# The last attention's loop: heavy rows in the middle, expert pieces spread evenly, and half of the edge features added by the gathers

## The chip, the core and the metric

The kernel runs on one core of one Trainium2 chip. The core has five engines with a queue of instructions each: PE (TensorE, matrix products), DVE (VectorE), ACT (ScalarE), POOL (GpSimd) and SP (SyncE, which here only issues transfers). Sixteen DMA engines move the data. The metric is device time in microseconds; the kernel before was run three times, with a median of 5483.48 us (5478.16 to 5485.61).

## What is computed

Four graph layers alternate with four expert layers on 3125 nodes of 256 features. The change lies in the last two, an attention over 50,000 edges sorted by destination, and a mixture of eight experts:

```python
def _L3_gnn_ref(x, edge_index, edge_attr, Wq, bq, Wk, bk, Wv, bv, We, Ws, bs):
    q, k, v = ...                       # x @ W + b, as (n, 8, 32)
    e = (edge_attr @ We).reshape(-1, H, C)
    kj = k[src] + e
    alpha = jnp.einsum('ehc,ehc->eh', q[dst], kj) / jnp.sqrt(jnp.float32(C))
    ...                                 # softmax of alpha over the edges of a destination
    msg = (v[src] + e) * alpha[:, :, None]
    out = jax.ops.segment_sum(msg, dst, num_segments=n)
    return out.reshape(n, H * C) + (x @ Ws + bs)

def _L3_ffn_ref(x, ...):
    w = jax.nn.softmax(jnp.mean(x, axis=0) @ Wr + br, axis=-1)
    h = jax.nn.relu(_bn(jnp.einsum('bfd,edh->bfeh', x, W1) + b1, ...))
    h = jax.nn.relu(_bn(jnp.einsum('bfeh,ehk->bfek', h, W2) + b2, ...))
    y = jnp.einsum('bfeh,ehd->bfed', h, Wo) + bo
    return jnp.einsum('bfed,fe->bfd', y, w)
```

The edge's feature row `e` is added both to the key and to the value of the edge's source.

## The kernel before, in words

**Rows and groups.** Both layers are one loop, in `gnn3_rows` (from line 1294). The nodes were sorted by how many edges come in. A tile holds 128 nodes, one to a partition; a step of a tile takes one edge for each of its nodes. The 25 light tiles have 5 to 31 steps. Nodes with 32 edges or more have their edges cut into heavy rows of 32 steps; there are three tiles of them. In all there are 440 steps, taken in 66 groups of at most eight (`GW`). The sums of the heavy rows are joined (`many_join`) before the last three light tiles, the ones whose nodes have heavy rows too, are begun.

**A group.** `fetch` (line 1391) puts on POOL's queue: for a tile's first group one gather of its queries, one gather of the features of all the group's steps (`e_`, one contiguous stretch of E to a partition), and one gather for each step, of the key and value rows of the edges' sources, 2 KB a partition (`kv`). POOL works through its queue in order. `kv` has three buffers and `e_` two. `ahead` copies the features of a pair of steps to PSUM on ACT, and `add` (line 1419) adds them to key and value on DVE. Then DVE multiplies by the query and sums by head (L1669, L1672), works out the running maximum, and, after ACT's exponential, multiplies the values by the weights (L1694). PE sums the group's weighted values in PSUM by products with an identity (L1633), in `sum_up`, which is called in the middle of the next group and which also fetches the group after that.

**The experts.** The light tiles form units of four (the last ones of two and one). When all tiles of a unit have their attention, `next_layer` hangs a chain of small tasks on `todo` (norm, transpose, gate), of which a few are done in each group; at its end the unit's expert work is put on `slots` as pieces: a product of a layer's half (its PSUM bank is read by a relu on ACT, L1575), or a result of two tiles (read by DVE, L1590, which weighs it and adds it to the nodes). `add` takes pieces from `slots` as its account `room` allows: each step pays in 1.25 and each group 1.5, and each piece costs what is written beside it. What is left when the loop ends is done behind it. Each unit loads all experts' weights anew on SP's queue.

**What sets the order.** The loop is under a manual schedule: DVE, ACT, PE and POOL each run their instructions in the order in which the program writes them, and wait by semaphores for each other.

Of the kernel before, what the change touches and what calls it, by code (L numbers as in the profile page):

```python
# [9 lines left out]
F32 = mybir.dt.float32  # L10
BF16 = mybir.dt.bfloat16
I32 = mybir.dt.int32
U32 = mybir.dt.uint32
AF = mybir.ActivationFunctionType
ALU = mybir.AluOpType
# [4 lines left out]
P = 128  # L20
C = 256
KC = C // P
N = 3125
NT = 25
# [3 lines left out]
GW = 8  # L28
# [4 lines left out]
HB = 3  # L33
# [25 lines left out]
class Kernel:  # L59
# [1234 lines left out]
    def gnn3_rows(self):  # L1294
# [4 lines left out]
        nc, tc, a, S = self.nc, self.tc, self.a, self.S  # L1299
        H, dh = 8, 32  # L1300
        QX = self.dram.tile([NP, 2, C], F32, name="r3_QX")
        KV = self.dram.tile([NP, 2, C], F32, name="r3_KV")
        row_of = lambda x: x.rearrange("n i c -> n (i c)")
        heads = lambda x: x.rearrange("p (h d) -> p h d", h=H)
        with pool_of(tc, name="r3t", bufs=1) as sp, pool_of(tc, name="r3tp", bufs=2, space=PSUM) as pp:
            w = sp.tile([P, KC, 4, C], F32, name="w4")
            b = sp.tile([P, 4, C], F32, name="b4")
            for i, x in enumerate("qskv"):
                nc.sync.dma_start(out=w[:, :, i, :], in_=a["L3_gnn_W" + x].rearrange("(k p) f -> p k f", p=P))
                ap = a["L3_gnn_b" + x]  # L1310
# [41 lines left out]

        fb = NT - HN

        units = [list(range(t, t + 4)) for t in range(0, fb - 2, 4)] + [[fb - 2, fb - 1], [NT - 1, fb], [fb + 1]]
        order = [HB + t for u in units[:-3] for t in u] + list(range(HB)) + [HB + t for u in units[-3:] for t in u]
        steps = [(i, s0, n, g) for i in order for g, (i_, s0, n) in enumerate(S.groups) if i_ == i]
        pairs = [(q, j) for q, (_, _, n, _) in enumerate(steps) for j in range(0, n, 2)]
        first_pair = [pairs.index((q, 0)) for q in range(len(steps))]
        unit_of = {t: u for u in units for t in u}  # L1360
        M0 = -0.1 * BIG
        with pool_of(tc, name="r3v", bufs=2) as vp, pool_of(tc, name="r3vp", bufs=2, space=PSUM) as pp, \
# [8 lines left out]
            got, todo, done, mvs, joined = {}, [], set(), {}, set()  # L1371
# [9 lines left out]
            def bank(shape, name):  # L1381

                while behind and behind[0][0] <= made[0] - 3:
                    _, ps, read = behind.pop(0)
                    read(ps)
                made[0] += 1
                return pp.tile(shape, F32, name=name, tag="bank", bufs=3)

            misc = lambda shape: bank(shape, f"misc{shape[0]}_{shape[-1]}_{len(shape)}")

            def fetch(q):
                if q >= len(steps):
                    return
                i, s0, n, g = steps[q]
                kv = vp.tile([P, GW, 2, C], F32, name="kv", bufs=3)
                e = vp.tile([P, GW, C], F32, name="e_", bufs=2)
                qx = None
                if s0 == 0 and HB <= i < HB + fb:
                    qx = vp.tile([P, 2 * C], F32, name="qx", bufs=2)
                    self.gather(qx, row_of(QX), S.id[:, i - HB : i - HB + 1])  # L1400
                self.gather(e[:, :n, :].rearrange("p n c -> p (n c)"), self.E, S.at[:, g : g + 1])
                for j in range(n):
                    o = S.start[i] + s0 + j
                    self.gather(kv[:, j].rearrange("p i c -> p (i c)"), row_of(KV), S.src[:, o : o + 1])
                got[q] = kv, e, qx

            copies, room = {}, [0.0]

            def ahead(p):

                if p >= len(pairs):
                    return
                q, j = pairs[p]
                n = min(2, steps[q][2] - j)
                pe = pp.tile([P, 2, C], F32, name="pe", bufs=2)
                nc.scalar.copy(pe[:, :n, :], got[q][1][:, j : j + n, :])
                copies[p] = pe

            def add(q, j):
                n = min(2, steps[q][2] - j)  # L1420
                room[0] += n * 1.25
                while slots and room[0] > 0:
                    room[0] -= slot()
                if not slots:
                    room[0] = 0.0
                p = first_pair[q] + j // 2
                kv = got[q][0][:, j : j + n]
                nc.vector.tensor_tensor(kv, kv, copies.pop(p)[:, :n, :].unsqueeze(2).to_broadcast([P, n, 2, C]), ALU.add)  # L1428
                ahead(p + 2)

            def many_join():
# [110 lines left out]
            def load(i):  # L1542

                if i >= len(units) * E // 2 or i in weights_of:
                    return
                weights_of[i] = []
                for e in (i * 2 % E, i * 2 % E + 1):
                    w = wp.tile([P, 3, KC, C], F32, name="w")
                    for k, x in enumerate(("W1", "W2", "Wo")):
                        nc.sync.dma_start(out=w[:, k], in_=a["L3_ffn_" + x][e].rearrange("(k p) f -> p k f", p=P))  # L1550
                    weights_of[i].append(w)

            def experts(u, hold):

                n = len(u) * P
                at = units.index(u) * E // 2
                for pair in range(E // 2):
                    es_ = (2 * pair, 2 * pair + 1)
                    h = {}

                    def product(e, l, f, pair=pair, h=h):
                        if l == 0 and f == 0:
                            load(at + pair + e % 2)
                        w = weights_of[at + pair][e % 2]
                        if f == 0:
                            h[e, l] = hp.tile([P, KC, 4 * P], F32, name=f"hT{l}")
                        x = hold["zT"] if l == 0 else h[e, 0]
                        ps = bank([P, 4 * P], "fp")
                        for k in range(KC):
                            nc.tensor.matmul(ps[:, :n], w[:, l, k, f * P : (f + 1) * P], x[:, k, :n], start=(k == 0), stop=(k == KC - 1))  # L1570
                        return ps

                    def relu(ps, e, l, f, h=h):
                        c = e * KC + f
                        nc.scalar.activation(h[e, l][:, f, :n], ps[:, :n], AF.Relu, bias=self.bn3[l][1][:, c : c + 1], scale=self.bn3[l][0][:, c : c + 1])  # L1575

                    def result(e, j0, pair=pair, h=h):
                        w = weights_of[at + pair][e % 2]
                        ps = bank([P, 4 * P], "fp")
                        for j in range(j0, min(j0 + 2, len(u))):  # L1580
                            for k in range(KC):
                                nc.tensor.matmul(
                                    ps[:, (j - j0) * C : (j - j0 + 1) * C], h[e, 1][:, k, j * P : (j + 1) * P], w[:, 2, k, :],
                                    start=(k == 0), stop=(k == KC - 1))
                        return ps

                    def weigh(ps, e, j0):
                        for j in range(j0, min(j0 + 2, len(u))):
                            x = self.xs[:, u[j], :]
                            nc.vector.scalar_tensor_tensor(  # L1590
                                x, ps[:, (j - j0) * C : (j - j0 + 1) * C], hold["g"][:, j, e : e + 1], x, op0=ALU.mult, op1=ALU.add)
                        if e == E - 1 and j0 + 2 >= len(u):
                            later.extend(u)

                    for l in range(2):
                        for e in es_:
                            for f in range(KC):
                                yield n / 512 * 1.75, lambda e=e, l=l, f=f, g=product: g(e, l, f), lambda ps, e=e, l=l, f=f, g=relu: g(ps, e, l, f)
                    for e in es_:
                        for j0 in range(0, len(u), 2):  # L1600
                            yield min(2, len(u) - j0) * 0.87, lambda e=e, j0=j0, g=result: g(e, j0), lambda ps, e=e, j0=j0, g=weigh: g(ps, e, j0)

            def slot():

                cost, make, read_ = slots.pop(0)
                if len(behind) > 1:
                    _, ps, read = behind.pop(0)
                    read(ps)
                ps = make()
                behind.append((made[0] - 1, ps, read_))  # L1610
                return cost
# [8 lines left out]
                        in_=self.xs[:n, t, :], in_offset=None)  # L1620

            load(0)
            fetch(0)
            fetch(1)
            for p in range(2):
# [16 lines left out]
            for st, (i, s0, n, g_) in enumerate(steps):  # L1642
                kv, e_, qx = got[st]
                light = i >= HB
                t = i - HB
                last = s0 + n == S.sizes[i]
                if s0 == 0:
# [9 lines left out]
                    if light and t >= fb:  # L1657
                        assert joined == set(range(HN))
                        m, den, before = tot[:, t - fb, C + H :], tot[:, t - fb, C : C + H], tot[:, t - fb, :C]
                room[0] += 1.5  # L1660


                for k, j in enumerate(range(added, n, 2)):
                    if k == 2:
                        sum_up(st)
                    add(st, j)
# [3 lines left out]
                l = vp.tile([P, H, GW + 1], F32, name="l")  # L1670
                ln = l[:, :, 1 : n + 1]
                nc.vector.tensor_reduce(ln, k_.rearrange("p n (h d) -> p h n d", h=H), AX.X, ALU.add)  # L1672
                o = S.start[i] + s0
# [9 lines left out]
                e = es[st % 2]  # L1683
# [56 lines left out]
            while todo or slots or behind or later:  # L1740
# [5 lines left out]
                if behind and not slots and not todo:  # L1746
                    _, ps, read = behind.pop(0)
# [672 lines left out]
```

## Time and profile before

| | us |
|---|---|
| median of three runs | 5483.48 (5478.16 to 5485.61) |
| the profiled execution, its time | 5477.25 |
| its span, first to last instruction | 5475.5 |
| first kv gather of the loop, last kv gather, last sum of the loop (start) | 4406.7, 5349.3, 5383.2 |
| busy over the whole span: PE, DVE, ACT, POOL | 2901.7, 3425.3, 1055.9, 3030.6 |

A stage is a stretch of the span, in microseconds from its start; its row gives how long each engine was busy in it. A group of instructions is a source line on an engine with its operands, its count, its busy time and the mean duration of one, and then how long the engine stood idle ahead of it and what ended that. The mean granted clock of TensorE is 0.74 over the span. The loop is the last fifth of it: what comes before does not change.

### The profile page before, as it was taken

What the parts mean: (1) busy time and instruction counts of PE and PEld (TensorE: products, weight loads), DVE (VectorE), ACT (ScalarE), POOL (GpSimd) and SP (SyncE); (2) the same over time, 40 slices, a digit from 0 to 9 for tenths busy, and PEclk for the clock granted to TensorE, in tenths of its full rate; (3) what the DMA queues carried; (4) which work ended last, traced back from release to release, by engine and by line L of the source; (5) the groups of instructions that cost most, each with busy time, mean ns of one, the idle gap of its engine ahead of it and who ended that gap; (6) DMA issues with size and microseconds to landing.
All of it is one profiled execution on the core that took longest, in us unless ns stands there. A gap on an engine that the chain in (4) does not pass through costs nothing. (4 is left out here: it accounts for less than half of the span.)

```text
span 5475.5 us, 41427 instructions
## 1 busy us (share of the span) xinstructions
PE 2901.7 (53%) x10276; PEld 2038.4 (37%) x10276; DVE 3425.3 (63%) x7869; ACT 1055.9 (19%) x2359; POOL 3030.6 (55%) x3128
## 2 busy tenths in 40 slices
PE   2233326962333258433332332888881637989858
PEld 1222225851222135322222221555551224656537
DVE  5998752126888645688847777211113677988893
ACT  1111101211111112211111110222221023433324
POOL 3777633024777431677747775677774054545550
PEclk9665657986656579755566565799995868999969
DMA  5677626743777400577737774232321566767764
GB/s 194 202 249 274 238 84 199 223 150 99 259 256 267 143 16 6 170 261 260 260 116 245 249 252 158 70 95 82 88 74 53 186 208 199 248 212 249 247 206 128
DMA packets 417368, 982.05 MB, mean 179 GB/s; under 512 B 98494, under 2 KB 238856, under 8 KB 386262
## 3 DMA queue, kind: packets, MB, share of 16 engines
q0 software_dynamic: 159856, 446.40, 27.8%
q1 hardware_dynamic: 229526, 468.51, 24.0%
q10 hardware_dynamic: 27728, 64.32, 3.0%
q8 instruction: 87, 1.43, 0.1%
q14 instruction: 171, 1.40, 0.1%
HBM read 629.95 MB, written 348.99 MB: 179 GB/s over the span
## 5 line engine op out<-in xcount | busy, mean ns | idle before, releaser
L1264 PE MATMUL fe_p<-feat_we,fe_T 128*128 128x256 f32 x1564 | 630.7, 573 | 1316.1 <-ACT fe_T L1260 1316.0
L1264 PEld LDWEIGHTS fe_p<-feat_we,fe_T 128*128 128x128 f32 x1564 | 434.8, 291 | 1476.2 <-ACT fe_T L1260 1380.8
L153 POOL DMA_INDIRECT hg<-g_H,A_src x782 | 760.3, 972 | 242.9 <-issue 210.4
L940 DVE SCALAR_TENSOR_TENSOR hg<-hg,A_keep,v 128x264 f32<-128x264 f32 (+1 forms) x1368 | 666.3, 487 | 44.8
L153 POOL DMA_INDIRECT hg<-f_H,B_src x512 | 520.0, 1016 | 156.1 <-issue 155.8
L153 POOL DMA_INDIRECT kv<-r_KV,r_src x440 | 417.9, 950 | 323.5 <-PE acc L1633 186.1
L932 DVE TENSOR_TENSOR v<-hg,e 128x1056 f32<-128x1056 f32 (+1 forms) x392 | 489.3, 1248 | 9.9 <-ACT e L924 3.6
L153 POOL DMA_INDIRECT hg<-g2a_H,A_src x391 | 373.5, 955 | 119.2 <-issue 104.9
L153 POOL DMA_INDIRECT hg<-g2b_H,A_src x391 | 370.8, 948 | 122.4 <-issue 103.1
L2229 DVE TENSOR_TENSOR l<-hg,ad 128x256 f32<-128x256 f32 x8 | 6.3, 789 | 571.0 <-DMA hg<-f_H,B_src 571.0
L924 ACT ACTIVATE e<-d 128x72 f32<-128x72 f32 (+1 forms) x196 | 43.3, 221 | 1596.6 <-DVE d L921 1596.5
L147 PE MATMUL tr<-ident,z 128*128 128x128 f32 x400 | 88.9, 352 | 395.7 <-DVE z L138 333.8
L1633 PE MATMUL acc<-kv,ident 128*128 128x256 f32 x880 | 238.7, 430 | 93.4 <-DVE kv L1694 93.4
L1428 DVE TENSOR_TENSOR kv<-kv,pe 128x1024 f32<-128x1024 f32 (+1 forms) x227 | 261.7, 1178 | 14.9 <-DMA kv<-r_KV,r_src 12.9
L2205 PE MATMUL ps<-zT,w 128*128 128x512 f32 (+1 forms) x448 | 202.6, 590 | 83.0 <-ACT hT L2206 82.9
L1633 PEld LDWEIGHTS acc<-kv,ident 128*128 128x128 f32 x880 | 193.3, 221 | 137.0 <-DVE kv L1694 97.7
L158 POOL DMA_INDIRECT A_Z<-D,A_first x100 | 98.8, 988 | 220.3 <-DVE hs_all L853 103.6
L147 PEld LDWEIGHTS tr<-ident,z 128*128 128x128 f32 x400 | 56.7, 176 | 429.1 <-DVE z L138 209.8
L153 POOL DMA_INDIRECT y<-f_Y,pos x50 | 47.4, 948 | 304.1 <-DMA arow<-in_L_gnn_a_src_dram 289.2
L1570 PE MATMUL fp<-zT,w 128*128 128x512 f32 (+2 forms) x512 | 192.2, 522 | 18.2 <-DVE xs L1590 6.0
L2210 PE MATMUL ps<-w,hT 128*128 128x256 f32 x800 | 199.2, 392 | 0.0
L1570 PE MATMUL fp<-hT,w 128*128 128x512 f32 (+2 forms) x512 | 190.8, 521 | 6.6 <-ACT hT L1575 5.5
(754 smaller groups left out, 6390.4 us busy)
## 6 DMA issues: line engine op xcount, KB each, us to landing
g_OUT<-hg SPq DMA_DIRECT2D x96, 1088.0 KB
g2a_OUT<-hg SPq DMA_DIRECT2D x48, 1088.0 KB
fe_a<-in_edge_attr_dram SPq DMA_DIRECT2D x97, 512.0 KB
E<-fe_o ACTq DMA_DIRECT2D x97, 512.0 KB
g2b_OUT<-hg SPq DMA_DIRECT2D x48, 1032.0 KB
w<-in_L_ffn_w_dram SPq DMA_DIRECT2D x80, 512.0 KB
w<-in_L_ffn_W_dram SPq DMA_DIRECT2D x128, 256.0 KB
w<-in_L_ffn_Wo_dram SPq DMA_DIRECT2D x64, 256.0 KB
```

Of the source, the lines that this page charges most:

```text
L147: nc.tensor.transpose(ps[:, k, :], z[:, t, k * P : (k + 1) * P], self.ident)
L153: return self.nc.gpsimd.indirect_dma_start(out=out, out_offset=None, in_=table, in_offset=bass.IndirectOffsetOnAxis(ap=idx, axis=0))
L158: i = self.nc.gpsimd.indirect_dma_start(out=table, out_offset=bass.IndirectOffsetOnAxis(ap=idx, axis=0), in_=in_, in_offset=None)
L924: nc.scalar.activation(e, d, AF.Exp)
L932: nc.vector.tensor_tensor(vals(v)[:, :k], vals(g[:, j0 : j0 + k, :W]), e[:, :, j0 + 1 : j0 + k + 1].rearrange("p h n -> p n h").unsqueeze( ...
L940: nc.vector.scalar_tensor_tensor(to, prev, L.keep[:, t + j0 + j : t + j0 + j + 1], v[:, j, :], op0=ALU.mult, op1=ALU.add)
L1264: nc.tensor.matmul(pe[:m, i, :], aT[:, i, k, :m], self.feat_we[:, k, :], start=(k == 0), stop=(k == KC - 1))
L1428: nc.vector.tensor_tensor(kv, kv, copies.pop(p)[:, :n, :].unsqueeze(2).to_broadcast([P, n, 2, C]), ALU.add)
L1570: nc.tensor.matmul(ps[:, :n], w[:, l, k, f * P : (f + 1) * P], x[:, k, :n], start=(k == 0), stop=(k == KC - 1))
L1633: nc.tensor.matmul(acc_, self.ident, x, start=(j == 0), stop=(j == len(terms) - 1))
L2205: nc.tensor.matmul(ps[:, :n], w1[:, k, f * P : (f + 1) * P], zT[:, k, b0 : b0 + n], start=(k == 0), stop=(k == KC - 1))
L2210: nc.tensor.matmul(po, hT[:, f, i * P : (i + 1) * P], w2[:, f, :], start=(f == 0), stop=False)
```

## The change

There are three edits. The first concerns the order: the three heavy tiles come after the first three units (12 light tiles) instead of after all but the last five tiles, and the three light tiles that need them come before the two of the last plain unit; the last units are now one of three tiles and one of two.

The second concerns the pace: each step pays into `room` the cost of the pieces that remain divided by the steps that remain (without the last unit, less 15), with other costs for the pieces; the 1.5 for each group is gone.

The third concerns the features: the first four steps of a group (`plain`) are done as before. Those of steps five to eight are gathered by a transfer of their own (`fetch_rest`, one group ahead, into the single buffer `er`), copied by ACT into both halves of the kv buffer, and the kv gathers of these steps add to what lies there (`compute_op`). `kv` has four buffers, and `e_` is half as long.

```diff
-        units = [list(range(t, t + 4)) for t in range(0, fb - 2, 4)] + [[fb - 2, fb - 1], [NT - 1, fb], [fb + 1]]
-        order = [HB + t for u in units[:-3] for t in u] + list(range(HB)) + [HB + t for u in units[-3:] for t in u]
+        units = [list(range(t, t + 4)) for t in range(0, fb - 2, 4)] + [[NT - 1, fb, fb + 1], [fb - 2, fb - 1]]
+        order = [HB + t for u in units[:3] for t in u] + list(range(HB)) + [HB + t for u in units[3:] for t in u]
...
-        pairs = [(q, j) for q, (_, _, n, _) in enumerate(steps) for j in range(0, n, 2)]
+        plain = [min(n, GW // 2) for _, _, n, _ in steps]
+        pairs = [(q, j) for q in range(len(steps)) for j in range(0, plain[q], 2)]
...
+            rest = {}
+            at2 = vp.tile([P, len(S.groups)], I32, name="at2", bufs=1)
+            nc.vector.tensor_scalar(at2, S.at, GW // 2, None, op0=ALU.add)
+            def fetch_rest(q):
+                if q < len(steps) and plain[q] < steps[q][2]:
+                    i, s0, n, g = steps[q]
+                    k = plain[q]
+                    e = rest[q] = vp.tile([P, GW // 2, C], F32, name="er", bufs=1)
+                    self.gather(e[:, : n - k, :].rearrange("p n c -> p (n c)"), self.E, at2[:, g : g + 1])
...
-                kv = vp.tile([P, GW, 2, C], F32, name="kv", bufs=3)
-                e = vp.tile([P, GW, C], F32, name="e_", bufs=2)
+                k = plain[q]
+                kv = vp.tile([P, GW, 2, C], F32, name="kv", bufs=4)
+                if k < n:
+                    nc.scalar.copy(kv[:, k:n], rest.pop(q)[:, : n - k, :].unsqueeze(2).to_broadcast([P, n - k, 2, C]))
+                e = vp.tile([P, GW // 2, C], F32, name="e_", bufs=2)
...
-                self.gather(e[:, :n, :].rearrange("p n c -> p (n c)"), self.E, S.at[:, g : g + 1])
+                self.gather(e[:, :k, :].rearrange("p n c -> p (n c)"), self.E, S.at[:, g : g + 1])
+                fetch_rest(q + 1)
                 for j in range(n):
                     o = S.start[i] + s0 + j
-                    self.gather(kv[:, j].rearrange("p i c -> p (i c)"), row_of(KV), S.src[:, o : o + 1])
+                    nc.gpsimd.indirect_dma_start(
+                        out=kv[:, j].rearrange("p i c -> p (i c)"), out_offset=None, in_=row_of(KV),
+                        in_offset=bass.IndirectOffsetOnAxis(ap=S.src[:, o : o + 1], axis=0),
+                        compute_op=ALU.add if j >= k else ALU.bypass)
...
+            left = [sum(len(u) for u in units[:-1]) * 8 * (1.23 + 0.77) - 15.0, S.total]
...
             def add(q, j):
                 n = min(2, steps[q][2] - j)
-                room[0] += n * 1.25
+                room[0] += n * left[0] / left[1]
+                left[1] -= n
                 while slots and room[0] > 0:
-                    room[0] -= slot()
+                    cost = slot()
+                    room[0] -= cost
+                    left[0] -= cost
                 if not slots:
                     room[0] = 0.0
+                if j >= plain[q]:
+                    return
...
-                                yield n / 512 * 1.75, lambda e=e, l=l, f=f, g=product: g(e, l, f), lambda ps, e=e, l=l, f=f, g=relu: g(ps, e, l, f)
+                                yield n / 512 * 1.23, lambda e=e, l=l, f=f, g=product: g(e, l, f), lambda ps, e=e, l=l, f=f, g=relu: g(ps, e, l, f)
...
-                            yield min(2, len(u) - j0) * 0.87, lambda e=e, j0=j0, g=result: g(e, j0), lambda ps, e=e, j0=j0, g=weigh: g(ps, e, j0)
+                            yield min(2, len(u) - j0) * 0.77, lambda e=e, j0=j0, g=result: g(e, j0), lambda ps, e=e, j0=j0, g=weigh: g(ps, e, j0)
...
+            fetch_rest(0)
             fetch(0)
...
-                room[0] += 1.5
```

More of the change, by code (lines that the diff above doesn't have):

```diff
@@ L1413, in ahead @@
                 q, j = pairs[p]
-                n = min(2, steps[q][2] - j)
+                if p in copies or q not in got:
+                    return
+                n = min(2, plain[q] - j)
                 pe = pp.tile([P, 2, C], F32, name="pe", bufs=2)
@@ L1420, in add @@
                 n = min(2, steps[q][2] - j)
-                room[0] += n * 1.25
+                room[0] += n * left[0] / left[1]
+                left[1] -= n
                 while slots and room[0] > 0:
-                    room[0] -= slot()
+                    cost = slot()
+                    room[0] -= cost
+                    left[0] -= cost
                 if not slots:
                     room[0] = 0.0
+                if j >= plain[q]:
+                    return
                 p = first_pair[q] + j // 2
+                ahead(p)
                 kv = got[q][0][:, j : j + n]
                 nc.vector.tensor_tensor(kv, kv, copies.pop(p)[:, :n, :].unsqueeze(2).to_broadcast([P, n, 2, C]), ALU.add)
+                ahead(p + 1)
                 ahead(p + 2)
```

## The prediction

> **What bounds the kernel now.** I read the stages first (busy time of each engine per 100 us of the last attention's loop), since a mean over 5.5 ms of other layers says nothing about this loop. The columns are microseconds of PE, weight loads, VectorE (DVE), ScalarE (ACT) and GpSimd (POOL), then the granted TensorE clock, the share of the DMA engines, and GB/s.
>
> ```profile
> 4700.00:4800.00 100.00, 96.43 (x343) 63.08 (x344) 92.53 (x149) 36.68 (x68) 60.43 (x64) 0.98 0.80 256
> 4900.00:5000.00 100.00, 96.39 (x338) 63.06 (x337) 96.38 (x146) 39.08 (x67) 59.15 (x62) 1.00 0.79 270
> 5100.00:5200.00 100.00, 83.74 (x297) 56.31 (x295) 84.75 (x118) 31.61 (x61) 55.79 (x58) 0.96 0.75 245
> 5200.00:5300.00 100.00, 48.58 (x136) 37.21 (x136) 94.63 (x141) 22.28 (x44) 54.04 (x57) 0.66 0.62 198
> 5300.00:5400.00 100.00, 76.37 (x297) 61.10 (x298) 71.83 (x129) 32.31 (x66) 29.70 (x31) 0.85 0.46 144
> 5400.00:5475.50 75.50, 68.54 (x375) 60.53 (x375) 13.75 (x35) 33.57 (x69) 5.50 (x5) 0.98 0.49 155
> ```
>
> From 4500 to 5200 PE and DVE are both nearly full. From 5200 the pieces of expert work have run out: DVE alone is full (95) and PE idles at clock 0.66. After 5400 it is the other way round: PE alone finishes the experts. So the loop has two bounds in turn, and a hole where they do not overlap. The groups of instructions in the window of the loop give the prices (busy, mean ns, then idle before):
>
> ```profile
> L153 POOL DMA_INDIRECT kv<-r_KV,r_src x440 | 417.9, 950 | 323.5 <-PE acc L1633 186.1 <-issue 105.5 <-PE misc L1492 11.5
> L1428 DVE TENSOR_TENSOR kv<-kv,pe 128x1024 f32<-128x1024 f32 x213 | 252.6, 1211 | 14.5 <-DMA kv<-r_KV,r_src 12.5 <-ACT pe L1416 1.9
> L1428 DVE TENSOR_TENSOR kv<-kv,pe 128x512 f32<-128x512 f32 x14 | 9.5, 678 | 0.4 <-DMA kv<-r_KV,r_src 0.4
> L1669 DVE TENSOR_TENSOR kv<-kv,q 128x2048 f32<-128x2048 f32 x44 | 100.6, 2287 | 1.6
> L1655 ACT COPY xs<-qx 128x256 f32<-128x256 f32 x22 | 8.8, 401 | 0.0
> ```
>
> The DVE hardly ever waits for a gather (12.5 us in the loop); POOL itself waits 186 us for PE to free a kv buffer. Next the order in time: POOL's gathers start every 1.25 us when nothing holds them, and PE without cover shows its back-to-back pace:
>
> ```profile
> 4714.20 0.95 POOL L153 DMA_INDIRECT kv<-r_KV,r_src  x1 [0.30 <-issue]
> 4715.45 0.95 POOL L153 DMA_INDIRECT kv<-r_KV,r_src  x1 [0.30 <-issue]
> ...
> 5416.19 3.62 PE L1570 MATMUL fp<-zT,w 128*128 128x256 f32 x16
> 5419.65 3.62 PE L1570 MATMUL fp<-hT,w 128*128 128x256 f32 x16
> 5423.10 3.62 PE L1582 MATMUL fp<-w,hT 128*128 128x256 f32 x16
> 5426.55 3.62 PE L1570 MATMUL fp<-zT,w 128*128 128x256 f32 x16
> ```
>
> Two experts of two tiles take 5426.55 - 5416.19 = 10.36 us, 2.59 per tile and expert; a 256-column matmul record takes 3.45 / 16 = 0.216 us. Last, the DMA queues between 4600 and 5200:
>
> ```profile
> q0 software_dynamic: 28669, 111.94, 57.2%
> q1 hardware_dynamic: 31008, 29.89, 15.1%
> ```
>
> POOL's gathers cost 0.572 x 600 / 111.94 = 3.07 us of all sixteen engines per MB, so a kv gather (128 rows of 2 KB, 0.262 MB) costs 0.80.
>
> **The change, part by part.**
>
> *VectorE.* 54 of the 66 groups have more than four steps. In them only the first two pairs are still added by DVE: 227 adds become 125. Of the 102 removed, 94 are full and 8 single: 94 x 1.211 + 8 x 0.678 = 119 us. DVE's busy time in the loop (the stages from 4400 to 5400) is 856, so 737 stay. One new add makes the shifted indices (some 0.2 us).
>
> *ScalarE.* It loses as many feature copies (102, about 58 us at 0.59) and gains 54 copies from SBUF into both halves of kv, up to 2048 elements. No row has that size: 0.40 us for 256 elements and 0.59 for 512 give 0.74 ns an element, so 1.7 us for a full one, 85 us in all. Net +27 on an engine about a third busy: nothing by itself. But the copy stands in ACT's queue ahead of the relus that empty PE's banks; from 0 to 54 x 1.7 = 92 us. I take 0, because two unread pieces (3.5 us of PE) cover 1.7 us; without that cover it would be the 92.
>
> *GpSimd.* Each of the 54 groups needs a second feature gather: 54 x 1.25 = 68 us. Its gathers and scatters for the loop go from 556 to 610, 697 to 765 us. Whether an adding gather also takes longer to issue is not in this trace: from the plain 0.95 us to an estimate of half more, 1.43 (a third address for each row), so 0 to 94 us in all; I take the middle, 47. This gives 812 us.
>
> *The waits.* A kv buffer is now the fourth, so the gathers' own wait for PE (186 us) reaches a group further back. In its place the second feature gather waits for ACT's copy, as its buffer is single. Behind it on POOL stand the eight kv gathers of a group two groups ahead, and behind those the next features; DVE's adds and its multiply wait for them. The copy comes early in group s (by the built order, after the bank reads of its first pieces): 3 us in at the worst, 2 for the copy, then nine issues of 1.25, so the last adding gather is out after 16 us and lands at about 20 (4.2 is the median now). The multiply of group s+2 comes two groups of at least 12.6 us later, at 26. So about 5 us to spare: I take 0. POOL's transfers use eight semaphores in turn, each transfer waiting for the eighth before it, so a landing of more than 8 x 1.25 = 10 us would stall POOL as well. At the start the first copy holds up the first kv gathers by about 4 us.
>
> *DMA engines.* Plain cost over the loop: 440 kv gathers 354 us, features 57.7 MB x 3.07 = 177, queries and results about 28, weights of seven units instead of eight (44 MB at 0.151 x 600 / 29.89 = 3.03) 134: 693 us. No adding transfer is in this trace. Lower bound: it costs what a plain one does, 693. The rule that speaks against the change is the Trainium skill's "Collectives: The Full Stack", "The bandwidth ceiling": adding in a DMA is slower not for the addition but because it takes two source reads, measured there as a ratio of 1.93. By that, 196 adding gathers cost 196 x 0.80 = 157 us more: 850. The upper end is a third access's worth, 1007. I take 850: an add must read the old contents, and the row alone can't show it.
>
> *Order and pace.* Heavy rows (12 groups) now stand after 12 light tiles, whose expert pieces cover them; the pace is what remains divided by the steps that remain, so the hole of 5200 to 5300 should close. PE's work from about 4515, when the first pieces come: experts 25 x 8 x 2.59 = 518 (seven units or eight make no difference by the pace above), 880 summing records x 0.216 = 190 less 21 done by then, small ones 48: 735 us. Between 4600 and 5200 the same count gives 525 us of back-to-back work in 600, 0.875.
>
> *The tail.* The last sum is at 5383 now, and the span ends 92 us later. After: some 20 us of pieces held back, the last unit's two tiles 8 x 2 x 2.59 = 41, waits of its chain 10, the end 7: 78.
>
> **The sum**, as the end of the span by each bound. PE: 4515 + 735 / 0.875 + 6 = 5361. DVE: 4407 + 737 / 0.875 + 78 = 5327. POOL: 4411 + 812 / 0.92 + 78 = 5372. DMA: 4407 + 850 / 0.95 + 78 = 5380 (0.80 is the most it shows in 100 us now; the 0.95 is my estimate for when it is the bound). The latest, with 5 us for four bounds so close together, is 5385; with the plain row for an adding gather it would be POOL's 5372 + 5. The profiled execution took 5477.25 with a span of 5475.5, and the median of the three runs is 6 above it: 5385 + 2 + 6 = **5393 us**, 1.7% faster.
>
> **The rivals.**
> (a) The add is nearly free for DMA and for POOL: PE alone bounds, at 0.90 to 0.93 now that DVE is lighter: 4515 + 735 / 0.92 + 6 + 8 = 5328, to 5350. For it: DVE's slack; against: a second read has to go somewhere.
> (b) POOL bounds with 1.43 us an adding gather: 4411 + 859 / 0.92 + 78 + 8 = 5431.
> (c) Little or no change: ACT's long copies and the POOL-to-ACT wait cost the relus their time (the 92 us): 5393 + 92 = 5485. Against it: ACT is a third busy.
> (d) Slower: the adding gathers make the DMA engines the bound. The loop has today's time when 4407 + x / 0.95 + 78 = 5475, so x = 940, which is reached when an adding gather costs 1 + (940 - 693) / 157 = 2.6 plain ones. At 3: 4407 + 1007 / 0.95 + 78 + 8 = 5553. For it: DMA is already 0.8 busy in the best stages, and long landings stall POOL through its eight semaphores; against: 2.6 is well over the two reads.
>
> **How the numbers follow.** A change under 0.2% (11 us) can't be told from none here. Likeliest case 0.47 (its own range 5350 to 5430), (a) 0.15, (b) 0.05, (c) 0.08 (half of it within 0.2%, a quarter on each side), (d) 0.25. Faster 0.47 + 0.15 + 0.05 + 0.02 = 0.69, the same 0.04, slower 0.25 + 0.02 = 0.27. The range goes from 5320, the lower end of (a), to 5510, which is an adding gather of 2.75 plain ones; what is left out is the far part of (d), about 0.15, and 0.03 below.
>
> **What would show it.** Right: 125 adds at L1461 and about 737 us of DVE in the loop; no 100 us stage without expert matmuls; DMA share over 0.9 in the middle; a landing of adding gathers under 9 us; POOL's kv wait for PE mostly gone. Wrong: DVE's multiply (L1703) waiting for kv gathers by more than 60 us in all; an adding gather's issue well over 1.4 us; a DMA share near 1 with fewer columns a microsecond than now; relus waiting behind L1413; a tail over 92 us.

## The result, and the profile after

The changed kernel takes 5494.51 us (median of 9 runs, 5489.15 to 5502.28), the kernel before 5479.66 beside it (9 runs, 5473.37 to 5485.61). The ratio is 1.0027, 95% interval 1.0017 to 1.0037: 0.27% slower, where the prediction had 5393. The profiled execution of the changed kernel has a span of 5492.7 us, 17.2 more than before.

For the experiments one thing must be known: those marked "late" below ran on cores where engines at times stood still with nothing to wait for, most of all in layers ahead of this loop, so that the kernel before took 6461 to 6491 us there (medians); a late run is compared only with the kernel before on the same cores.

The first view is the stages of the loop, with the columns of the prediction's (busy PE, weight loads, DVE, ACT, POOL; clock, DMA share, GB/s).

```profile
4700.00:4800.00 100.00, 93.81 (x336) 61.65 (x335) 74.98 (x113) 37.42 (x57) 74.95 (x64) 0.98 0.89 231
4900.00:5000.00 100.00, 81.33 (x278) 55.07 (x277) 81.76 (x130) 38.05 (x56) 78.98 (x70) 0.93 0.94 257
5000.00:5100.00 100.00, 64.46 (x213) 43.34 (x212) 76.08 (x128) 28.20 (x48) 74.11 (x65) 0.80 0.82 203
5200.00:5300.00 100.00, 85.83 (x275) 54.03 (x276) 67.80 (x118) 36.84 (x51) 70.22 (x61) 0.93 0.81 210
5300.00:5400.00 100.00, 83.86 (x301) 57.85 (x300) 62.18 (x104) 28.44 (x46) 33.99 (x30) 0.93 0.54 147
5400.00:5492.70 92.70, 78.70 (x339) 62.38 (x337) 18.71 (x56) 31.40 (x55) 5.42 (x5) 0.95 0.24 75
4400.00:5400.00 1000.00, 763.15 (x2589) 504.80 (x2590) 737.57 (x1227) 348.11 (x541) 696.52 (x605) 0.88 0.82 217
```

From 4700 to 4800 PE is nearly as full as before (94 of 100); from 4900 on no engine looks like the bound. DVE has fallen, from 92 to 96 of 100 to 75 to 82, as meant. POOL stands at 74 to 79, but its own pause of 0.30 us after each gather isn't counted as busy. POOL's queue shows that (start, duration, idle before):

```profile
4707.94 0.98 POOL L153 DMA_INDIRECT e__37737<-E,r_at  x1 [0.30 <-DVE d L1716]
4709.23 0.96 POOL L153 DMA_INDIRECT er<-E,at  x1 [0.30 <-issue]
4710.49 0.95 POOL L1423 DMA_INDIRECT kv<-r_KV,r_src  x1 [0.30 <-issue]
...
4715.50 1.58 POOL L1423 DMA_INDIRECT kv<-r_KV,r_src  x1 [0.30 <-issue]
4717.38 1.55 POOL L1423 DMA_INDIRECT kv<-r_KV,r_src  x1 [0.30 <-issue]
4719.23 1.54 POOL L1423 DMA_INDIRECT kv<-r_KV,r_src  x1 [0.30 <-issue]
4721.07 1.53 POOL L1423 DMA_INDIRECT kv<-r_KV,r_src  x1 [0.30 <-issue]
```

An overwriting gather starts every 1.25 us (the one behind 4710.49 is at 4711.75, not shown), an adding one every 1.85: it holds POOL for 1.55 us where a plain one takes 0.95. The groups in the window of the loop and the first and last kv gather and sum:

```profile
L1423 POOL DMA_INDIRECT kv<-r_KV,r_src x440 | 536.2, 1219 | 138.1 <-issue 116.4 <-PE acc L1668 4.9 <-ACT kv L1413 4.7
L1413 ACT COPY kv<-er 128x2048 f32<-128x2048 f32 x44 | 83.3, 1894 | 8.5 <-DMA er<-E,at 6.2 <-DMA qx<-r_QX,r_id 2.0 <-DMA kv<-r_KV,r_src 0.3
L153 POOL DMA_INDIRECT er<-E,at x54 | 51.3, 950 | 78.3 <-ACT kv L1413 47.6 <-ACT small L1718 12.2 <-issue 11.3
L1423 POOL DMA_INDIRECT kv<-r_KV,r_src x440: 942/953/1671, 4410.4 to 5341.8; - x147
L1668 PE MATMUL acc<-kv,ident x880: 378/380/797, 4429.0 to 5414.9; 128*128 128x256 f32 x176
```

The kv gathers keep POOL busy for 118 us more (536.2 for 417.9), which is 196 adding ones at 0.60. POOL's wait for PE is gone (4.9 us, 186.1 before). Of POOL's 610 gathers and scatters 594 lie between the first and the last kv gather: 594 x 1.25 + 196 x 0.60 = 860 us of 931.4, or 0.92. Most of the rest is the wait of `er`, 62 us beyond its pauses, of which ACT's copy ended 47.6. So POOL, with that one wait in it, is the bound as long as it gathers. Yet its last gather is 7.5 us earlier than before; the loss comes behind it. From the last gather to the last sum it was 33.9 us and is 73.1.

What lies there? PE's queue at the end of the loop shows the unit of the three late tiles begin (384 columns), then DVE's queue follows:

```profile
5362.49 0.69 PE L1564 MATMUL misc<-bo,gT 8*128 8x256 f32 x2
5363.11 5.43 PE L1604 MATMUL fp<-zT,w 128*128 128x384 f32 x16
...
5375.47 1.35 DVE L1624 SCALAR_TENSOR_TENSOR xs<-fp,g,xs 128x256 f32<-128x256 f32 x3 [11.26 <-PE fp L1616]
5378.06 1.35 DVE L1624 SCALAR_TENSOR_TENSOR xs<-fp,g,xs 128x256 f32<-128x256 f32 x3 [1.24 <-PE fp L1616]
5390.97 0.88 DVE L1624 SCALAR_TENSOR_TENSOR xs<-fp,g,xs 128x256 f32<-128x256 f32 x2 [11.56 <-PE fp L1616]
5391.76 1.21 DVE L1461 TENSOR_TENSOR kv<-kv,pe 128x1024 f32<-128x1024 f32 x1
```

The unit of the three late tiles gets its pieces only at 5363. All steps but a few have been paid for by then, so the pace puts the unit's pieces into the last adds of the loop, and DVE stands twice for over 11 us at results of experts, in front of the attention's own work. POOL's DMA queue between 4600 and 5200 (packets, MB, share of 16 engines):

```profile
q0 software_dynamic: 42083, 114.68, 74.5%
```

And PE's expert products (tile `fp`) in the stretches that held a hole. Columns: length, busy PE, then clock, DMA share and GB/s of the core. First of the kernel before, then of the changed one:

```profile
5160.00:5180.00 20.00, 12.35 (x40) 0.94 0.65 202
5180.00:5200.00 20.00, 1.32 (x7) 0.91 0.75 239
5200.00:5320.00 120.00, 0.00 (x0) 0.67 0.64 203
```

```profile
4980.00:5040.00 60.00, 0.21 (x1) 0.74 0.85 227
5180.00:5220.00 40.00, 4.69 (x21) 0.83 0.86 211
5340.00:5360.00 20.00, 0.00 (x0) 0.68 0.37 114
```

Taken from the start of one expert product to the start of the next, the one hole of 145.7 us (from 5180.9) has become three: 75.9 us (from 4979.8), 34.9 (from 5186.1) and 30.4 (from 5332.7), 141.2 together. The first comes behind the heavy tiles. Their 12 groups (DVE's multiplies from 4660 to 4838) end no light tile, so no unit gives new pieces; those of the first three units last until 4980, and the fourth unit's begin only at 5055.7. The second and the third end in the same way, with the next unit's first piece.

### The profile page after: what moved, and what is told of

The parts are those of the page before. It is cut to its first block, busy times and chain, and to the rows that moved or that the text cites. A ratio compares the mean times of both kernels' runs of the same rounds, so it can differ in the third digit from the quotient of the medians.

```text
span 5492.7 us, 41104 instructions
## 1 busy us (share of the span) xinstructions
PE 2898.2 (53%) x10148; PEld 2024.2 (37%) x10148; DVE 3312.0 (60%) x7761; ACT 1076.8 (20%) x2274; POOL 3192.3 (58%) x3182
## 3 DMA queue, kind: packets, MB, share of 16 engines
q0 software_dynamic: 179408, 446.40, 30.4%
## 5 line engine op out<-in xcount | busy, mean ns | idle before, releaser
L1423 POOL DMA_INDIRECT kv<-r_KV,r_src x440 | 536.2, 1219 | 138.1 <-issue 116.4
L153 POOL DMA_INDIRECT hg<-f_H,B_src x512 | 519.0, 1014 | 156.1 <-issue 155.7
L1616 PE MATMUL fp<-w,hT 128*128 128x256 f32 x800 | 189.3, 391 | 15.6 <-ACT hT L1609 12.2
```

The lines of the kernel that those rows point to most:

```text
L153: return self.nc.gpsimd.indirect_dma_start(out=out, out_offset=None, in_=table, in_offset=bass.IndirectOffsetOnAxis(ap=idx, axis=0))
L1423: nc.gpsimd.indirect_dma_start(out=kv[:, j].rearrange("p i c -> p (i c)"), out_offset=None, in_=row_of(KV), in_offset=bass.IndirectOffsetO ...
L1616: nc.tensor.matmul(ps[:, (j - j0) * C : (j - j0 + 1) * C], h[e, 1][:, k, j * P : (j + 1) * P], w[:, 2, k, :], start=(k == 0), stop=(k == K ...
```

## The experiments

Theories. **P**: the loss is made by the new order and pace, and the adding gathers are worth about nothing. **G**: order and pace gain, and the adding gathers cost more than DVE saves. **D**: the second read of an adding gather makes the DMA engines the bound. The edits are shown against the changed kernel; lines that only adapt indices and the feature buffers to them are left out.

**Order and pace alone.** All features are added by DVE again.

```diff
-        plain = [min(n, GW // 2) for _, _, n, _ in steps]
+        plain = [n for _, _, n, _ in steps]
-                kv = vp.tile([P, GW, 2, C], F32, name="kv", bufs=4)
+                kv = vp.tile([P, GW, 2, C], F32, name="kv", bufs=3)
```

> Only the new order and pace, all features added on VectorE (the chip of the first four runs stalled every engine's instruction supply, 18% on the whole kernel, so the four are looked at again). Theory G (the adding gathers make POOL the loop's bound): 5420 to 5460. Theory P (the order and pace leave PE without pieces): 5485 or more.

Measured: 5496.36, ratio to the kernel before on the same cores (5482.14) 1.0025 [1.0015, 1.0036]. The whole loss is there without a single adding gather, as P has it; order and pace don't gain, so G's first half falls. Its own gathers and sums:

```profile
L1422 POOL DMA_INDIRECT kv<-r_KV,r_src x440: 942/948/1182, 4410.8 to 5350.7; - x147
L1667 PE MATMUL acc<-kv,ident x880: 379/379/796, 4429.0 to 5420.5; 128*128 128x256 f32 x176
```

From first to last gather 939.9 us (942.6 before), from there to the last sum 69.8 (33.9), from there to the end 74.9 (92.3). The tail gains 17 (14 were predicted), and the stretch ahead of it loses 36. The same kernel had a late run, with this expectation:

> Only the new order and pace; all features are added on VectorE as before the change (three kv buffers, full e_). Theory G (the gathers that add cost 1.55 us of POOL instead of 0.95, which with 54 more feature gathers makes POOL the bound of the loop, 610 x 1.25 + 196 x 0.6 = 883 us): POOL is back at 697 us of cycles, VectorE at 856, and the time falls below the kernel before, 5420 to 5460. Theory P (the new order and pace leave PE without pieces around 5000 to 5065 and again before the last unit, whatever the gathers do): 5485 or more.

It came to 0.9993 [0.9977, 1.0009].

**What the adding gathers gain and cost.** Three kernels with the new order and pace. In the first, the gathers of steps five to eight overwrite, so that the features of these steps are left out: it keeps ACT's copies, the second feature gathers and DVE's relief, and drops the adding itself.

```diff
-                        compute_op=ALU.add if j >= k else ALU.bypass)
+                        compute_op=ALU.bypass)
```

> The changed kernel with overwriting instead of adding gathers (the features of steps five to eight are left out of the result). Theory G and theory D (the second read of the DMA engines): 5400 to 5440, the last kv gather 60 to 100 us after the loop's start earlier than now. Theory P: 5480 or more.

Measured: 5446.78, ratio 0.9937 [0.992, 0.9953], between the two ranges; the last kv gather is 51.5 us earlier, at 5290.3, where 60 to 100 were expected. The second is the same with POOL's time put back by two fills of a small tile behind each of these gathers:

```diff
+            fill = vp.tile([P, 224], F32, name="fill", bufs=1)
...
+                    if j >= k:
+                        nc.gpsimd.memset(fill, 0.0)
+                        nc.gpsimd.memset(fill, 0.0)
```

> Overwriting gathers with two small memsets on POOL behind each of the 196 (features of steps five to eight left out): the POOL time of adding without the second read. Theory G: within 15 us of the changed kernel, 5475 to 5505. Theory D: as the overwriting kernel, 5400 to 5440.

Measured: 5477.88, ratio 0.9992 [0.9983, 1.0]: in the range of G, and D falls. The kv gathers of the first, then a stretch of POOL's queue of the second:

```profile
L1423 POOL DMA_INDIRECT kv<-r_KV,r_src x440 | 417.9, 950 | 152.2 <-issue 114.0 <-ACT kv L1413 12.5 <-PE acc L1668 10.5
```

```profile
4698.08 0.95 POOL L1424 DMA_INDIRECT kv<-r_KV,r_src  x1 [0.15 <-issue]
4699.02 0.30 POOL L1429 MEMSET fill<- 128x224 f32 x1
4699.39 0.28 POOL L1430 MEMSET fill<- 128x224 f32 x1
4699.83 0.95 POOL L1424 DMA_INDIRECT kv<-r_KV,r_src  x1 [0.16 <-issue]
```

A gather and its fill take 1.75 us, 0.10 less than an adding gather: 98 of the 118 us are put back. From kernel to kernel, by the medians: without adding gathers 5496; with free ones 5447, so DVE's relief is worth some 50 us; with POOL's time 5478, so this costs 31; with the add itself 5494.5, another 17 to 19. The steps lie in the stretch from the first to the last kv gather, 939.9, 874.9, 913.2 and 931.4 us; what follows it is 145 in the first and 151 to 155 in the others. In the last step the stretch grows by 18 us, POOL lacked 20 us in the kernel with fills, and POOL's wait for ACT's copy is 47.6 us in both. So POOL's time is enough to explain it, and nothing needs to be left for the second read of the DMA; that a part of it is this read can't be excluded. The relief and the price come out even.

The relief isn't DVE's adds alone: the three kernels also have the fourth kv buffer, where the one with order and pace alone has three. What that buffer is worth by itself was not tried.

Both also had a late run. The overwriting one:

> The changed kernel, but the kv gathers of steps five to eight overwrite instead of adding (the features of these steps are left out of the result; feature gather and ScalarE copy stay). This takes away both the longer issue on POOL and the second read by the DMA engines. Theory G, and theory D (the second read makes the DMA engines the bound): POOL falls to 765 us, the last kv gather is about 60 to 100 us earlier than 5342, the time is 5400 to 5440. Theory P: the holes stay, 5480 or more.

Measured 1.0193 [1.0148, 1.0238], but its loop took 1243 us there from first gather to end, 1030 on the cores of the other run: it is stretched by stops with nothing to wait for, and nothing is read from it. The one with fills:

> As the kernel whose kv gathers overwrite, plus two small POOL memsets (some 0.29 us each by the rows of POOL's memsets, 0.21 for 128 elements) behind each of the 196 gathers: the POOL time of the adding gathers without their second read. The features of steps five to eight are left out. Theory G: as the changed kernel, 5475 to 5500. Theory D: as the overwriting kernel, 5400 to 5440.

Measured 1.0008 [0.9986, 1.0029].

**Half as many adding gathers.** Only steps seven and eight are added by gathers, 92 instead of 196.

```diff
-        plain = [min(n, GW // 2) for _, _, n, _ in steps]
+        plain = [min(n, GW - 2) for _, _, n, _ in steps]
-                    e = rest[q] = vp.tile([P, GW // 2, C], F32, name="er", bufs=1)
+                    e = rest[q] = vp.tile([P, 2, C], F32, name="er", bufs=1)
...
-                    scaled = vp.tile([P, C], F32, name="scaled")
+                    scaled = vp.tile([P, C], F32, name="scaled", bufs=1)
```

The last pair takes one buffer away from the rescaled sum, to make room for the longer `e_`.

> Only steps seven and eight of a group get their features through adding gathers (92 instead of 196, in 48 groups instead of 54); steps one to six are added on VectorE; one buffer less for the rescaled sum to make room. POOL: 697 + 48 x 1.25 + 92 x 0.6 = 812 us, VectorE 856 - 56 = 800. Theory G: between the changed kernel and the one with order and pace alone, 5440 to 5475. Theory P: 5485 or more.

Measured: 5466.01, ratio 0.9971 [0.9961, 0.998]: faster than both kernels by more than the intervals, and the best of the kernels that leave nothing out, late runs aside. The number lies in G's range, but not where G put it, between two kernels that came to 5494.5 and 5496.4. And P falls here with its second half: some adding gathers are worth something.

```profile
L1423 POOL DMA_INDIRECT kv<-r_KV,r_src x440 | 472.9, 1075 | 135.4 <-issue 107.5 <-DMA kv<-r_KV,r_src 7.9 <-PE acc L1668 5.8
L1423 POOL DMA_INDIRECT kv<-r_KV,r_src x440: 942/946/1586, 4408.0 to 5315.5; - x147
L1668 PE MATMUL acc<-kv,ident x880: 379/379/796, 4426.4 to 5389.4; 128*128 128x256 f32 x176
```

The last gather comes 26 us earlier than in the changed kernel: 104 adding gathers fewer free 62 us of POOL, and DVE takes back 54 adds (63 us) that it has room for. The 73.9 us from the last gather to the last sum are unchanged.

**Order from pace.** The order of before with the new pace and costs, and the reverse; all features added by DVE.

```diff
-        units = [...] + [[NT - 1, fb, fb + 1], [fb - 2, fb - 1]]
+        units = [...] + [[fb - 2, fb - 1], [NT - 1, fb], [fb + 1]]
-        order = [HB + t for u in units[:3] for t in u] + list(range(HB)) + [HB + t for u in units[3:] for t in u]
+        order = [HB + t for u in units[:-3] for t in u] + list(range(HB)) + [HB + t for u in units[-3:] for t in u]
```

> The new pace and the new costs of the pieces alone: order and units of before, all features added by VectorE. If the loss of 14 us of order and pace together sits in the pace, 5495; if it sits in the order, 5480 or less; if spreading the pieces closes the hole of 5200 to 5300, 5450 to 5460.

```diff
-                room[0] += n * left[0] / left[1]
+                room[0] += n * 1.25
-                                yield n / 512 * 1.23, ...
+                                yield n / 512 * 1.75, ...
-                            yield min(2, len(u) - j0) * 0.77, ...
+                            yield min(2, len(u) - j0) * 0.87, ...
+                room[0] += 1.5
```

> The new order of tiles and units alone: pace and costs of the pieces of before, all features added by VectorE. If the loss sits in the order (the last unit of two plain tiles gets its chain of small tasks only behind the last gathers, and the heavy tiles are joined late for the unit of three), 5495 to 5510; if it sits in the pace, 5480 or less.

All of these runs were late. The others of pace alone:

> The new pace and the new costs of the pieces alone: order and units of before, all features added by VectorE. If the loss of 14 us sits in the pace, 5495; if it sits in the order, 5480 or less, and if spreading the pieces closes the hole of 5200 to 5300, 5460.

> The new pace and the new costs of the pieces alone: order and units of before, all features added by VectorE. The run of this kernel among cores whose instructions came late gave 0.995 of the kernel before, which can't be carried over. If the loss of 14 us of order and pace together sits in the pace, 5495; if it sits in the order, 5480 or less; if spreading the pieces closes the hole of 5200 to 5300, 5450 to 5460.

In this order, with the one above last: 0.9949 [0.9935, 0.9963], 0.9929 [0.9905, 0.9953] and 0.9933 [0.9911, 0.9954]. The other of order alone:

> The new order of tiles and units alone: pace and costs of the pieces of before, all features added by VectorE. If the loss of 14 us sits in the order (the last unit of two plain tiles gets its chain of small tasks late), 5495; if it sits in the pace, 5480 or less.

It had 1.0021 [0.9997, 1.0046], the one above 1.0012 [0.9994, 1.003]. The size can't be carried over: order and pace together were 0.9993 late and 1.0025 else. The sign agrees with what the profiles show of the pieces. Expert products of the order alone, then of the pace alone:

```profile
5920.00:6040.00 120.00, 0.00 (x0) 0.66 0.68 210
6200.00:6220.00 20.00, 0.00 (x0) 0.67 0.68 220
```

```profile
6215.00:6255.00 40.00, 0.00 (x0) 0.67 0.57 175
```

The order alone has the hole of before in another place, adds a second of 20 us, and leaves more for the end: 112.6 us from the last sum. The pace alone shortens the one hole to these 40 us and most of the 20 on either side (3.55 and 2.75 us of expert products), and has 39.3 us from the last gather to the last sum (6302.0 to 6341.3) and 74.4 from there to the end. The gathers and sums of the order alone, then of the pace alone:

```profile
L1422 POOL DMA_INDIRECT kv<-r_KV,r_src x440: 940/946/1519, 5366.7 to 6358.9; - x147
L1667 PE MATMUL acc<-kv,ident x880: 379/379/796, 5384.5 to 6390.3; 128*128 128x256 f32 x176
```

```profile
L1422 POOL DMA_INDIRECT kv<-r_KV,r_src x440: 940/947/1525, 5341.6 to 6302.0; - x147
L1667 PE MATMUL acc<-kv,ident x880: 376/379/796, 5359.4 to 6341.3; 128*128 128x256 f32 x176
```

Side by side, in us ("experts there" is how long PE is busy with expert products behind the last gather; the last column is the sum of all gaps of over 12 us between the starts of neighbouring expert products, in the whole loop):

| order | pace | last gather to last sum | last sum to end | both | experts there | without expert products |
|---|---|---|---|---|---|---|
| before | before | 33.9 | 92.3 | 126.2 | 98.6 | 145.7 |
| new | new | 69.8 | 74.9 | 144.7 | 107.3 | 155.7 |
| new | before | 31.4 | 112.6 | 144.0 | 117.0 | 173.0 |
| before | new | 39.3 | 74.4 | 113.7 | 82.9 | 92.8 |

The last two rows come from late runs, but these stretches hardly depend on that: the late run of order and pace has 69.7 and 74.9, and the other late runs of order and of pace alone agree within 2 us. So it is the order that costs at the end, 18 us with the pace of before and 31 with the new one. The pace only decides on which side of the last sum this work falls; by itself, in the order of before, it saves 12.5 us there and over a third of the hole. The expert products show what costs: the new order leaves 18 us more of them behind the last gather with the pace of before, and 24 more with the new pace.

**The adding gathers alone**, with the order and pace of before.

> Adding gathers for the features of steps five to eight, with the order and the pace of before. If the loss of 0.27% is all in order and pace and the adding gathers are worth about nothing (theory P), 5470 to 5490. If the gathers show their worth with the old order (theory G), 5440 to 5465. If the adding gathers alone are a loss, 5500 or more.

(G stands there for the gathers' worth showing with the old order.) The three runs ahead of it:

> Only the adding gathers; order, pace and piece costs are those before the change. Theory G: POOL's 883 us bound the loop, so VectorE's 119 us less bring nothing: 5480 to 5520. Theory P: without the new holes VectorE's gain shows, 5380 to 5440.

> Adding gathers for the features of steps five to eight, with the order and the pace of before. If the loss of 0.27% is all in order and pace and the adding gathers are worth about nothing (theory P), 5470 to 5490: no change from the kernel before. If the gathers only show their worth with the old order, because the pieces then fill the stretch that the lighter VectorE opens (theory G), 5440 to 5465. If the adding gathers alone are a loss, 5500 or more.

> Adding gathers for the features of steps five to eight, with the order and the pace of before. If the loss of 0.27% is all in order and pace and the adding gathers are worth about nothing (theory P), 5470 to 5490. If the gathers show their worth with the old order (theory G), 5440 to 5465. If the adding gathers alone are a loss, 5500 or more.

All late, in this order and the one above last: 0.9982 [0.9962, 1.0002], 0.9988 [0.9973, 1.0003], 0.9971 [0.9959, 0.9984] and 0.9978 [0.9964, 0.9992]. A gain of 0.1 to 0.3% there, with two of the four intervals reaching 1, so not a loss; on other cores it wasn't measured. 33.7 us from the last gather to the last sum, 94.8 from there to the end: both as in the kernel before, so that neither the new gap nor the new tail is the gathers' doing.

**Two adding steps in the order of before.** Two steps added by gathers with the order of before and the new pace:

> Only steps seven and eight of a group are added by gathers (5466 us with the new order and pace), with the new pace and the order and units of before. If the order costs some 14 to 25 us, 5440 to 5452; if the order costs nothing, 5466.

Measured late: 1.0068 [1.0039, 1.0096]. With order and pace of before:

> Only steps seven and eight of a group are added by gathers, as in the kernel with two added steps (5466 us with the new order and pace), and the order and pace are those of before. If the order and the pace cost their 0.25% here too, 5452. If they help as soon as VectorE is lighter (the stretch without expert work then costs less), 5470 to 5485.

Measured late: 1.017 [1.0138, 1.0202]. Both are slower, against what was expected, and that isn't explained. Their loops are stretched (1166 and 1209 us, 1086 to 1108 with four adding steps) by stops with nothing to wait for, but the order alone has such stops too (PE stands 57 and 74 us in this way at the weighted sums, 60 in the order alone). So the gain of two adding steps is shown for the new order and pace only.

## Why the prediction was wrong

Its sum by POOL was 4411 + 812 / 0.92 + 78 = 5372. Measured are the same terms: the last gather at 5341.8 instead of 5294 (+48), then 73 that the sum hasn't got, then 78. That is 5294 + 48 + 73 + 78 = 5493, the span. Two steps failed.

*"Order and pace: the hole should close."* It split and stayed as large, 141.2 us for 145.7, and a stall grew behind the last gather. Order and pace alone give 1.0025, the whole change 1.0027. The step counted only how many pieces there are and how many steps pay for them; it didn't ask when a unit's pieces exist. The heavy groups bring none, and those of the unit of three come when next to no step is left, so that they are paid at once, ahead of the last sums. That this falls ahead of the last sums is the pace's doing; that it falls behind the last gather at all is the order's (144 us there with either pace, 126.2 before). The sum held a simpler fault too: it put the tail straight behind the last gather, though the table of before shows 33.9 us between them (5349.3 to 5383.2). With these 34 the POOL bound would have read 5406; the other 39 are the new stall, of which the shorter tail, which the prediction had, gives back 14.

*GpSimd's adding issue.* Taken as 0.95 us plus a middle of 0.24, bounded at 1.43 by an estimate. It is 1.55, outside the bounds: 880 us instead of 812. The prediction put all 610 gathers and scatters into the stretch; counted in its way, POOL's share is 880 / 931.4 = 0.945, better than the 0.92 used, and this is the +48. With 880 and the 34 the POOL bound would have been 4411 + 880 / 0.945 + 34 + 78 = 5454.

What held:
- VectorE: 737 us predicted, 737.57 measured between 4400 and 5400, with 125 adds.
- The tail of 78 us: 77.8.
- The second read. Order and pace alone has 61.9% of 600 us for 118.14 MB in queue 0, 3.14 us per MB. At this the 114.68 MB of the changed kernel would take 360 us; they took 447. The 87 fall on some 282 x 196 / 440 = 126 adding gathers: 0.69 on 0.82, or 1.84 plain ones; the kernel with two adding steps, worked out in the same way, gives 0.71. This is an estimate. The Trainium skill's ratio of 1.93 ("Collectives: The Full Stack", "The bandwidth ceiling") was the right choice against the plain row (the 157 us were a ratio of 2; 1.93 makes 146); but with a DMA share of 0.82 over the loop (0.94 in its fullest 100 us) and POOL's time enough for the stretch of the gathers, no run shows the DMA as the bound.
- ScalarE's full copy: 1.7 us predicted, 1.89 measured.

What was taken as 0 and is not: the second feature gather waits 47.6 us for ACT's copy, where 5 us were to spare. And ACT itself waits for POOL, which the prediction didn't name:

```profile
5061.17 1.90 ACT L1413 COPY kv<-er 128x2048 f32<-128x2048 f32 x1 [1.17 <-DMA er<-E,at]
...
5075.06 0.59 ACT L1443 COPY pe<-e__39587 128x512 f32<-128x512 f32 x1 [10.29 <-DMA e__39587<-E,r_at]
5075.59 0.37 ACT L1689 COPY q<-qx 128x256 f32<-128x256 f32 x1
...
5076.20 1.44 ACT L1609 ACTIVATE hT<-fp,bn 128x512 f32<-128x512 f32 x2
```

```profile
5075.99 2.29 DVE L1703 TENSOR_TENSOR kv<-kv,q 128x2048 f32<-128x2048 f32 x1 [9.03 <-ACT q L1689]
```

The next group's feature gather goes out only at 5070.43, since it stands behind four adding gathers in POOL's queue, without a pause longer than 0.30 us between them. ACT's feature copy waits for it, and behind this copy stand the query copy and the relus. DVE's multiply waits 38.5 us in all for query copies, in eight of nine cases in this way (37.7 us), and PE waits 36.3 us for relus (10.7 before), mostly in the same way. So the long copy of 1.89 us is not what holds them; POOL's lateness reaches DVE and PE through ACT's queue.

The rivals: (a), an add nearly free, fell with the 1.55 us; with free adds the time is 5447, not 5328 to 5350; the gathers still take 875 us, and the 75 us behind them stay. (b) was the right mechanism for the stretch of the gathers, with issue and gap too small. (c) came near in time (5485) by the wrong cause. (d), a DMA-bound loop, was not reached: 1.84 plain costs, not 2.6.

What stays open: what pace alone is worth on cores that are not late, where it wasn't measured, and why two adding steps were slower in the order of before. To hold back the unit of three until after the last sums needn't gain the 39 us: in the order alone its pieces come mostly there, and what is saved ahead of the last sum is lost behind it.

## What to carry to other kernels

When filler work is spread over a loop, look first at when it becomes available: an order that makes the last portions larger and later costs at the end, whatever the pace. A pace of "what remains by steps that remain" then pours the late portion ahead of the last results, and a slower one leaves it behind them. When a queue works in order, a late transfer holds up all that stands behind the first instruction that waits for it, here the query copies and the relus behind a feature copy. When an operation is moved from a compute engine into a transfer, price the issuing engine first; here 0.60 us for each of 196 gathers ate a relief of some 50 us, and moving half as many beat both kernels. Sum a chain through to the end: the stretch from the last transfer to the last result belongs in it.

## What was not expected of the hardware

An indirect gather of 128 rows of 2 KB that adds to what lies in SBUF holds POOL for 1.53 to 1.58 us instead of 0.95, with the same pause of 0.30 us behind it; two kernels agree on 0.60 us each (196 of them: 118.3 us more; 92 of them: 55.0). The landing changed less. Over the loop's kv gathers, first before, then after:

```profile
DMA to landing us min/median/max: 3.3/3.8/7.9
```

```profile
DMA to landing us min/median/max: 3.5/5.0/8.0
```
